# A third Strassen level in five more pairs of steps

## The chip, the cores and the metric

The kernel runs on one core of a Trainium2 chip. The metric is the device time in microseconds of one execution. TensorE (PE in the profile) does the matmuls, VectorE (DVE) and ScalarE (ACT) work on its results in PSUM, GpSimd (POOL) adds and subtracts tiles in SBUF and issues some DMAs, and SyncE (SP) issues most of the DMAs.

## The reference

All data are float32. `x` is 32 samples x 128 channels x 2048 positions. Two blocks follow each other, each added to its input:

```python
# block 0: per-sample channel mix, then a wide linear layer
h    = gelu(gelu(cond @ W0 + b0) @ W1 + b1)
att  = softmax(h @ W2 + b2)                        # 8 expert kernels
mix  = einsum('bk,koi->boi', att, weight)          # 128 x 128 for each sample
y    = einsum('boi,bih->boh', mix, x) + att @ bias_k
W'   = W + sum_e coeffs_e * scales_e * Bf_e @ A_e  # 2048 x 2048, 16 updates of rank 16
x    = x + y @ W'.T + bias                         # the reference adds the updates apart
# block 1: grouped convolution, then 16 small FFNs over permuted positions
z    = conv1d(x, 4 groups, 9 taps) + ctx + fside
t    = z[:, :, perm] in 16 heads of 128
x    = x + unpermute(gelu(t @ up) @ down)          # 128 -> 512 -> 128
```

The channel mix and the linear layer commute, so the kernel multiplies `x` by `W'` first (2048 x 2048 with 4096 rows) and mixes the channels of the product afterwards.

## The kernel before

The product with `W'` is the largest part: it fills the first half of the time. The rows of `x` (4096 = 32 samples of 128) are cut into 8 groups g = 0 to 7 of 4 samples, 512 rows each. The product is computed in Strassen's (Winograd's) form at two or three levels:

- **Rounds.** At the outer level the 2048 x 2048 product is 7 products of half size, the rounds `ROUNDS = P1, P2, P6, P7, P5, P3, P4`. Each round goes over the 8 groups: 56 *steps* i = (round r, group g).
- **Second level.** Within a step, `multiply` computes seven products named P1 to P7 again. Each is 4 matmuls of 128x128 weights against 512 columns that add up in one PSUM bank (L346). Products share banks: P1, P6, P7 and P4 add up in `px`, P5 and P3 in `py`, P2 has `pz`; between two of them the bank is read out. Where a partial result of an earlier round was loaded, DVE adds each bank to it (L339); in round P1 there is none, and the first write of each quarter of the new tile `m_rg` is a copy by ACT (L341). At the end the tile is stored to DRAM (`part_store`, L274, issued on SP).
- **Third level.** For a *pair* of steps (g even, then g odd), `multiply_third` leaves the second level's products P2 and P4 out of both steps and computes them for both together by seven *quarter* products, each 4 matmuls of 256 columns (`quarter`, L449, its result added by DVE, L457), all in the odd step, scattered between the plain products (L438, L434). The even step's tile is held until the odd step has ended (`held`). The quarters need combined weights, made once in a round (`third_weights`: two tiles `r_q0`, `r_q1`; eight POOL operations of 128x256, L390 to L396, and four of DVE, L1109), and combined inputs, made once for each pair (`third_inputs`: one tile `sq_i`, four operations of 128x512, L416 to L419, on POOL, or on DVE for a round's first pair). Before the change 19 pairs have it: all four of P6, P7, P5 and P3 and three of P2 (`THIRD`, `SKIP`).

The first round does more than its products. `W'` is made in 16 blocks of 1 MB (`w_khohkc`): loaded by SP (`w_load`, L161, two blocks in each step for the next one), the rank-16 updates multiplied on TensorE and added by DVE (`w_make_two`, 14 matmuls of 512 columns for two blocks, L220 and L223, ahead of the products of steps 1 to 5), summed by rows on DVE (`row_sums`, L240), and stored for the later rounds by a DMA that POOL issues (`w_store`, L165, to `wb_d`). At the start POOL also makes P1's inner weights (`inner_weights`, L249 to L253). A *chain* of small steps for the second half (`small`) advances after each step: after step 6 DVE works out positions (L927 to L935) and transposes and reduces the weights' sums through a tile `wsq` (L945, L946).

The last round, P4, mixes the channels (ACT, POOL and DVE, L566 to L584) and runs the first parts of the convolution between its steps. The convolution (L673), and the 128 FFN heads (L817, L828) fill the second half.

What sets the order: the program is scheduled by hand. The order of the code is the order of instructions on each engine and each queue, and an engine never passes a waiting instruction. In each step's code, first the next step's x is loaded (`x_load`, L265, SP) and combined (`x_combine`, L308 to L311, POOL); then come the step's `W'` blocks and their stores; then its products, with `between(j)` called after the j-th for what is to lie among them; then the store of the result, and the chain.

Nearly all large tiles (x, `W'` blocks, combined weights and inputs, partial results, `wsq`, tables) share one pool of `SLOTS` = 25 buffers of 1 MB (128 partitions x 2048 floats):

```python
def slot(name, shape=(P, L)):
    return big.tile(list(shape), FP, name=name, tag="s")
```

A new tile gets the next buffer, and its first writer waits until all users of that buffer's former tile are done. PSUM has 8 banks, handed out in turn by `bank()` and given back by `done()`.

Of the kernel before, what the change touches and what calls it, by code (L numbers as in the profile page):

```python
# [11 lines left out]
ALU = mybir.AluOpType  # L12
# [4 lines left out]
P = 128  # L17
B = 32
L = 2048
QW = 512  # L20
# [7 lines left out]
NQ = QW // 2  # L28
# [19 lines left out]
ROUNDS = ("P1", "P2", "P6", "P7", "P5", "P3", "P4")  # L48


THIRD = ("P2", "P6", "P7", "P5", "P3")
SKIP = (("P2", 3),)


@with_exitstack
def adaln_ffn_kernel(
# [16 lines left out]
    nc = tc.nc  # L73
# [8 lines left out]
    def slot(name, shape=(P, L)):  # L82
        return big.tile(list(shape), FP, name=name, tag="s")


    def bank():
        return banks.pop(0)

    def done(*ps):
        banks.extend(ps)  # L90

    def halves(t):
        return [t[:, r * NQ : (r + 1) * NQ] for r in range(2)]
# [144 lines left out]
    def row_sums(oh, t):  # L238
        for ki in range(2):
            nc.vector.tensor_tensor(wsum[:, oh], wsum[:, oh], t[:, ki], ALU.add)  # L240
# [32 lines left out]
    def part_store(n, g, t, eng=nc.gpsimd):  # L273
        eng.dma_start(part_d[n, g], t.rearrange("p k s c -> p (k s c)"))  # L274
# [129 lines left out]
        return quarters, ops  # L404

    def in_pair(r, g):
        return r in THIRD and (r, g // 2) not in SKIP

    def third_inputs(i, eng):

        (x11, x12), (x21, x22) = (
            [xa[n][:, 1, :, h * NQ : (h + 1) * NQ] for h in range(2)] for n in (i, i + 1)
        )
        tt = eng.tensor_tensor
        t = slot(f"sq_{i}", (P, 4, 2, NQ))
        tt(t[:, 0], x21, x22, ALU.add)  # L416
        tt(t[:, 1], t[:, 0], x11, ALU.subtract)
        tt(t[:, 2], x11, x21, ALU.subtract)
        tt(t[:, 3], x12, t[:, 1], ALU.subtract)  # L419
        return {  # L420
            "P1": x11, "P2": x12, "P3": t[:, 3], "P4": x22,
            "P5": t[:, 0], "P6": t[:, 1], "P7": t[:, 2],
        }

    def multiply_third(r, g, lhs, rhs, olds, between, quarters, sq):

        px, py = bank(), bank()
        if sq:
            qx, qy, qz = bank(), bank(), bank()
            both = [held.pop(), olds]  # L430

        def add(si, oi, ps):
            for acc in olds:
                nc.vector.tensor_tensor(acc[:, si, oi], ps, acc[:, si, oi], ALU.add)  # L434

        def product(k, ps, first, last):
            for kc in range(4):
                nc.tensor.matmul(  # L438
                    ps, lhsT=lhs[k][:, bass.ts(kc, P)], rhs=rhs[k][kc],
                    start=first and kc == 0, stop=last and kc == 3, skip_group_check=True,  # L440
                )

        def quarter(k, ps, first, last, *to):

            if not sq:
                return
            for i, out in enumerate(halves(ps)):
                for kc in range(2):
                    nc.tensor.matmul(  # L449
                        out, lhsT=sq[k][:, i, bass.ts(kc, P)], rhs=quarters[i][k][kc],  # L450
                        start=first and i == 0 and kc == 0, stop=last and i == 1 and kc == 1,
                        skip_group_check=True,
                    )
            for b, h in to:
                for acc in both[b]:
                    part = acc[:, :, 0, h * NQ : (h + 1) * NQ]
                    nc.vector.tensor_tensor(  # L457
                        part, ps.rearrange("p (s n) -> p s n", s=2), part, ALU.add
                    )

        product("P1", px, True, False)
        add(0, 0, px)
        between(0)
        quarter("P1", qx if sq else None, True, False, (0, 0))
        quarter("P2", qz if sq else None, True, True, (0, 0))
        if sq:
            done(qz)
        product("P5", py, True, False)
        add(1, 1, py)
        between(1)  # L470
        quarter("P6", qx if sq else None, False, False, (0, 1))
        quarter("P5", qy if sq else None, True, False, (1, 1))
        product("P6", px, False, False)
        add(0, 1, px)
        between(2)
        quarter("P7", qx if sq else None, False, False, (1, 1))
        quarter("P3", qy if sq else None, False, True, (0, 1))
        if sq:
            done(qy)
        product("P3", py, False, True)  # L480
        add(0, 1, py)
        done(py)
        between(3)
        quarter("P4", qx if sq else None, False, True, (1, 0))
        if sq:
            done(qx)
        product("P7", px, False, True)
        add(1, 1, px)
        add(1, 0, px)
        done(px)  # L490
        between(4)
        between(5)
        if not sq:
            held.append(olds)
            return
        for b, accs in enumerate(both):
            for (_, new), acc in zip(ADDED[r], accs):
                part_store(new, g - 1 + b, acc, nc.sync)

    held = []  # L500
# [345 lines left out]
    def late_loads():  # L846
        late["tw"] = slot("tw_l", (P, 4, GR, P))
        nc.sync.dma_start(late["tw"].rearrange("p k r c -> p (k r c)"), tw_d)
        late["w1"] = slot("w1", (P, NPH, QW))
        nc.sync.dma_start(late["w1"].rearrange("p f n -> p (f n)"), w1_d.to_broadcast([P, L]))  # L850
        late["fb"] = slot("fb", (P, NPH, QW))
        nc.sync.dma_start(
            late["fb"].rearrange("p f n -> p (f n)"), fbias.to_broadcast([P, L])
        )
# [161 lines left out]
    first = [wt.pop(k) for k in blocks[0:4]]  # L1016
# [15 lines left out]
    rhs = inner_weights("P1", first, make_first)  # L1032
    a_load(1, 0, 4)
    unsummed, unsummed_first = [], list(first)
    olds = {}
    chain = small()
    nxt, waiting, ts = {}, {}, {}
    heads = [(g, h) for g in range(NG) for h in range(NH)]

    def olds_load(i):  # L1040
# [3 lines left out]
    for i, (r, g) in enumerate(steps):  # L1044
        ri = i // NG
        last_round = ri + 1 == len(ROUNDS)
        if i + 1 < len(steps):
            if i + 1 not in xs:
                xs[i + 1] = x_loads(*steps[i + 1])
            if not last_round:  # L1050
                lhs[i + 1] = x_combine(*steps[i + 1], xs.pop(i + 1))
                if r in THIRD and g == 0:
                    quarters, quarter_ops = third_weights(r, rhs)
                if in_pair(r, g) and g % 2 == 0 and g > 0 and r != "P6":
                    sq = third_inputs(i, nc.gpsimd)
# [7 lines left out]
        if g == NG - (1 if ri else 2) and ri < len(ROUNDS) - 1:  # L1063
            nxt = inner_weights(ROUNDS[ri + 1], [nxt[kc] for kc in range(4)])
# [18 lines left out]
        elif ri + 1 < len(ROUNDS):  # L1083
            for k, combine in waiting.items():
                nxt[k] = combine()
            waiting = {}
            if 2 <= g < 6:
                waiting[g - 2] = outer_weights(ROUNDS[ri + 1], g - 2)

        if last_round and g == 0:  # L1090
            late_loads()
        if last_round and g == 2:

# [6 lines left out]
        def between(j):  # L1100

            b = (ri - 1) * (NG - 2) + g + 1 if ri > 0 else g - (NG - 2)
            if (g in range(1, NG - 1) if ri > 0 else g >= NG - 2) and b < B and j < KEXP // 2:
                mixed_kernel(b, (2 * j, 2 * j + 1))
            if ri == 0 and j == 2:
                for k in blocks[6 + 2 * g : 8 + 2 * g]:
                    wt[k] = w_load(*k)
            if r in THIRD and j < 4 and quarter_ops:
                nc.vector.tensor_tensor(*quarter_ops.pop(0), ALU.subtract)  # L1109
            if j == 3 and ahead and steps[i + 2][0] == "P6":  # L1110
                xs[i + 2] = x_loads(*steps[i + 2])
            if ri == 0 and j in (1, 3) and unsummed:
                row_sums(*unsummed.pop())
            if ri == 0 and j == 5 and unsummed_first:
                t = unsummed_first.pop(0)
                tt = nc.vector.tensor_tensor
                tt(wsum[:, 0, 0], wsum[:, 0, 0], t[:, 0, 0], ALU.add)
                tt(wsum[:, 0], wsum[:, 0], t[:, 1], ALU.add)
            if last_round:
                if j == 3 and i + 1 < len(steps):  # L1120
                    lhs[i + 1] = x_combine(*steps[i + 1], xs.pop(i + 1))
                    olds_load(i + 1)
                if j == 4 and i + 2 < len(steps):
                    xs[i + 2] = x_loads(*steps[i + 2])
                if j in (2, 4):
                    stage(k0 + j // 2, stage_first)
                if j % 2:
                    stage_third(k0 + j // 2)
                else:
                    stage(k0 + j // 2, stage_second)  # L1130
# [5 lines left out]
        else:  # L1136
            multiply(r, g, lhs.pop(i), rhs, olds.pop(i), between)
        xa.pop(i - 1, None)
        if in_pair(r, g) and g % 2 == 0 and (g == 0 or r == "P6"):
            sq = third_inputs(i, nc.vector)  # L1140
        next(chain, None)
        if i > 5:
            next(chain, None)
# [5 lines left out]
        if g == NG - 1 and ri + 1 < len(ROUNDS):  # L1149
            rhs = nxt  # L1150
            nxt = {}
# [86 lines left out]
```

## Time and profile before

| | before |
|---|---|
| median of 3 runs | 2592.68 us (2592.53 to 2594.41) |
| profiled execution | 2592.81 us |
| its span in the trace | 2591.0 us (1.8 us lie around it) |
| mean granted TensorE clock | 0.999 |
| PE busy | 2579.3 us, 6926 matmul records |
| DVE busy | 1491.7 us |
| POOL busy | 1329.8 us |
| ACT busy | 532.8 us |

The groups of instructions that the change touches, with all their busy time (a matmul's record contains a modelled tail, so records overlap):

| group | records | mean |
|---|---|---|
| L438, plain products in steps of a pair, two of its groups | 608 and 512 | 592 ns |
| L346, plain products elsewhere, its largest group | 288 | 592 ns |
| L308, POOL, combining x, the first of its four operations | 56 | 1319 ns |
| L434, DVE, adding a bank to u | 192 | 686 ns |

A float32 matmul is two records. The time of an engine in the page is a mean over the span; the first round lies from 46 to 303 us, the rounds up to P4 from there to 1232.7 us.

### The profile page before, as it was taken

The numbers are of one execution on the slowest core, as the hardware profiler recorded it, in microseconds if no ns is written. First come the engines' busy times: TensorE is split into PE (matmuls) and PEld (weight loads), VectorE is DVE, ScalarE is ACT, GpSimd is POOL, SyncE is SP. The second block draws the span as 40 slices with busy tenths as digits, with TensorE's granted clock in tenths as the row PEclk, the third lists the DMA queues.
The fourth block names the chain that finished last, engine by engine and source line by source line (L and its number), as shares of the span: only waits on it lengthen the run. The fifth ranks groups of instructions, "written<-read, shape, count | busy, mean of one in ns | idle before, by whom it ended". The sixth has DMA issues, their size and how long they took to land. (4 is left out here: it accounts for less than half of the span.)

```text
span 2591.0 us, 21495 instructions
## 1 busy us (share of the span) xinstructions
PE 2579.3 (100%) x6926; PEld 1314.6 (51%) x6926; DVE 1491.7 (58%) x2345; ACT 532.8 (21%) x1099; POOL 1329.8 (51%) x1096
## 2 busy tenths in 40 slices
PE   9999999999999999999999999999999999999999
PEld 4444455455555555555454455555555555455543
DVE  5654655466554666654276666667666666666601
ACT  0000000000000000000011244444444444444432
POOL 7320657888977845977314234343344334434222
PEclk9999999999999999999999999999999999999999
DMA  7543458779467477573866897777777877787432
GB/s 324 210 171 115 156 230 319 305 295 353 169 253 288 195 319 288 208 318 146 279 203 228 246 304 260 244 247 226 220 234 239 254 237 221 222 257 231 163 128 89
DMA packets 186576, 608.28 MB, mean 235 GB/s; under 512 B 17632, under 2 KB 91872, under 8 KB 142304
## 3 DMA queue, kind: packets, MB, share of 16 engines
q1 hardware_dynamic: 147936, 473.48, 50.9%
q0 software_dynamic: 32704, 130.04, 14.8%
q10 hardware_dynamic: 5824, 3.40, 0.4%
q8 instruction: 55, 0.90, 0.1%
q14 instruction: 57, 0.47, 0.1%
HBM read 372.45 MB, written 200.84 MB: 221 GB/s over the span
## 5 line engine op out<-in xcount | busy, mean ns | idle before, releaser
L817 PE MATMUL bank<-t,ws 128*128 128x512 f32 x1024 | 460.6, 592 | 0.4 <-DMA ws<-in_ffw 0.4
L828 PE MATMUL bank<-gl,ws 128*128 128x512 f32 x1024 | 460.2, 592 | 0.0
L835 POOL DMA_INDIRECT out<-t,orow x128 | 150.3, 1174 | 552.9 <-DVE t L833 470.6
L820 ACT ACTIVATE gl<-bank 128x512 f32<-128x512 f32 x512 | 305.9, 598 | 418.7 <-PE bank L817 408.5
L828 PEld LDWEIGHTS bank<-gl,ws 128*128 128x128 f32 x1024 | 194.6, 190 | 233.0 <-issue 231.5
L817 PEld LDWEIGHTS bank<-t,ws 128*128 128x128 f32 x1024 | 194.4, 190 | 227.6 <-issue 224.2
L566 POOL TENSOR_TENSOR x<-x,fb 128x512 f32<-128x512 f32 x128 | 176.7, 1409 | 236.9 <-DMA x<-in_x 217.7
L833 DVE TENSOR_TENSOR t<-bank,t 128x512 f32<-128x512 f32 x128 | 88.4, 690 | 326.7 <-PE bank L828 320.6
L438 PE MATMUL bank<-P_t,s_P 128*128 128x512 f32 x608 | 270.2, 592 | 0.0
L572 ACT ACTIVATE bank<-w,aggb 128x512 f32<-128x512 f32 x128 | 80.9, 684 | 849.9 <-DMA w<-w_d 832.5
L434 DVE TENSOR_TENSOR u<-bank,u 128x512 f32<-128x512 f32 x192 | 125.9, 686 | 212.9 <-PE bank L438 197.6
L438 PE MATMUL bank<-wo_P,s_P 128*128 128x512 f32 x512 | 227.6, 592 | 0.0
L280 POOL TENSOR_TENSOR xt<-xt,xt 128x512 f32<-128x512 f32 x128 | 164.5, 1317 | 97.3 <-DMA xt<-in_xT 97.2
L308 POOL TENSOR_TENSOR s_P<-xt 128x512 f32<-128x512 f32 x56 | 73.8, 1319 | 234.7 <-DMA xt<-in_xT 231.7
L545 DVE SCALAR_TENSOR_TENSOR ags<-mix,att_bc,ags 128x128 f32<-128x128 f32 x224 | 179.5, 801 | 4.7
L438 PEld LDWEIGHTS bank<-P_t,s_P 128*128 128x128 f32 x608 | 115.5, 190 | 129.2 <-issue 125.3
L801 POOL DMA_INDIRECT t<-hx_d,row x128 | 131.0, 1023 | 55.2 <-issue 27.0
L438 PEld LDWEIGHTS bank<-wo_P,s_P 128*128 128x128 f32 x512 | 97.3, 190 | 108.8 <-issue 106.2
L346 PE MATMUL bank<-P_t,s_P 128*128 128x512 f32 x288 | 126.5, 592 | 0.0
L673 PE MATMUL bank<-va,tw_l 128*128 128x256 f32 x512 | 122.3, 380 | 2.7 <-DVE va L657 2.6
L434 DVE TENSOR_TENSOR p<-bank,p 128x512 f32<-128x512 f32 x84 | 56.6, 688 | 116.7 <-PE bank L438 112.2
L673 PEld LDWEIGHTS bank<-va,tw_l 128*128 128x128 f32 x512 | 96.7, 190 | 45.3 <-issue 33.3
(188 smaller groups left out, 3558.9 us busy)
## 6 DMA issues: line engine op xcount, KB each, us to landing
xt<-in_xT SPq DMA_DIRECT2D x88, 1024.0 KB
u<-u_d SPq DMA_DIRECT2D x40, 1024.0 KB
wo_P<-wb_d SPq DMA_DIRECT2D x36, 1024.0 KB
u<-c_d SPq DMA_DIRECT2D x64, 512.0 KB
x<-in_x SPq DMA_DIRECT2D x32, 1024.0 KB
xg<-x SPq DMA_DIRECT2D x256, 128.0 KB
hx_d<-x1t SPq DMA_DIRECT2D x32, 1024.0 KB
hx_d<-ht SPq DMA_DIRECT2D x32, 1024.0 KB
```

The source lines that it names most:

```text
L280: nc.gpsimd.tensor_tensor(out[:, i, j], a[:, i, j], b[:, i, j], op)
L346: nc.tensor.matmul(ps, lhsT=lhs[k][:, bass.ts(kc, P)], rhs=rhs[k][kc], start=first and kc == 0, stop=last and kc == 3, skip_group_check=True,)
L434: nc.vector.tensor_tensor(acc[:, si, oi], ps, acc[:, si, oi], ALU.add)
L438: nc.tensor.matmul(ps, lhsT=lhs[k][:, bass.ts(kc, P)], rhs=rhs[k][kc], start=first and kc == 0, stop=last and kc == 3, skip_group_check=True,)
L545: nc.vector.scalar_tensor_tensor(ag, mix[:, k], att, ag, ALU.mult, ALU.add)
L566: nc.gpsimd.tensor_tensor(xt[:, f], xt[:, f], late["fb"][:, f], ALU.add)
L673: nc.tensor.matmul(out, lhsT=w[:, 2 * i + r], rhs=rhs, start=first and r == 0, stop=last and r == 1, skip_group_check=True,)
L801: nc.gpsimd.indirect_dma_start(out=t.rearrange("p k t -> p (k t)"), out_offset=None, in_=hx_d[g].rearrange("l k t -> l (k t)"), in_offset= ...
L817: nc.tensor.matmul(pu, lhsT=w[:, m * P : (m + 1) * P], rhs=t[:, 0], start=True, stop=True)
L820: nc.scalar.activation(gl[m], pu, AF.Gelu)
L828: nc.tensor.matmul(pd, lhsT=w[:, (MC + m) * P : (MC + m + 1) * P], rhs=gl[m], start=(m == 0), stop=(m == MC - 1),)
L835: nc.gpsimd.indirect_dma_start(out=out, out_offset=bass.IndirectOffsetOnAxis(ap=orow[:, g, h : h + 1], axis=0), in_=t[:, 1], in_offset=None,)
```

## The change

`THIRD` and `SKIP` give way to a table `PAIRS` of the pairs that have the third level. New in it are all four pairs of round P1 and the first pair of P4: 24 pairs instead of 19. In P1 and P4 (`ENDS`) the seven quarter products of the odd step stand behind its plain products instead of between them, and the combined inputs are always made on GpSimd. Since P1 has no partial results to add to, `multiply_third` now also takes a new tile `m_rg` and has ACT copy first writes into it, as `multiply` did. PSUM banks for quarters are taken when the first quarter of a bank comes. In P4, `third_weights` is issued at the start of the round's first step, behind the x that was combined before. The code below leaves out the old calls of `quarter` and unchanged lines.

```diff
-THIRD = ("P2", "P6", "P7", "P5", "P3")
-SKIP = (("P2", 3),)
+PAIRS = {
+    "P1": (0, 1, 2, 3), "P2": (0, 1, 2), "P6": (0, 1, 2, 3), "P7": (0, 1, 2, 3),
+    "P5": (0, 1, 2, 3), "P3": (0, 1, 2, 3), "P4": (0,),
+}
+ENDS = ("P1", "P4")
...
     def in_pair(r, g):
-        return r in THIRD and (r, g // 2) not in SKIP
+        return g // 2 in PAIRS[r]
...
     def multiply_third(r, g, lhs, rhs, olds, between, quarters, sq):
         px, py = bank(), bank()
+        accs = olds if olds[0] is not None else [slot(f"m_{r}{g}", (P, 2, 2, QW))]
+        fresh = set()
         if sq:
-            qx, qy, qz = bank(), bank(), bank()
-            both = [held.pop(), olds]
+            both = [held.pop(), accs]
         def add(si, oi, ps):
-            for acc in olds:
-                nc.vector.tensor_tensor(acc[:, si, oi], ps, acc[:, si, oi], ALU.add)
+            for acc in accs:
+                to = acc[:, si, oi]
+                if olds[0] is not None or (si, oi) in fresh:
+                    nc.vector.tensor_tensor(to, ps, to, ALU.add)
+                else:
+                    nc.scalar.copy(to, ps)
+            fresh.add((si, oi))
...
+        turns = [
+            (("P1", (0, 0)), ("P2", (0, 0))), (("P6", (0, 1)), ("P5", (1, 1))),
+            (("P7", (1, 1)), ("P3", (0, 1))), (("P4", (1, 0)),),
+        ]
+        def turn(n, now):
+            if sq and now:
+                for k, to in turns[n]:
+                    quarter(k, to)
+        early = r not in ENDS
         product("P1", px, True, False)
         add(0, 0, px)
         between(0)
+        turn(0, early)
         product("P5", py, True, False)
         add(1, 1, py)
         between(1)
+        turn(1, early)
         product("P6", px, False, False)
         add(0, 1, px)
         between(2)
+        turn(2, early)
         product("P3", py, False, True)
         add(0, 1, py)
         done(py)
         between(3)
+        turn(3, early)
         product("P7", px, False, True)
         add(1, 1, px)
         add(1, 0, px)
         done(px)
+        turn(0, not early)
         between(4)
+        turn(1, not early)
+        turn(2, not early)
         between(5)
+        turn(3, not early)
...
-                if r in THIRD and g == 0:
+                if g == 2 * PAIRS[r][0]:
                     quarters, quarter_ops = third_weights(r, rhs)
...
         if last_round and g == 0:
+            quarters, quarter_ops = third_weights(r, rhs)
             late_loads()
...
-            if r in THIRD and j < 4 and quarter_ops:
+            if j < 4 and quarter_ops:
                 nc.vector.tensor_tensor(*quarter_ops.pop(0), ALU.subtract)
...
-        if in_pair(r, g) and g % 2 == 0 and (g == 0 or r == "P6"):
-            sq = third_inputs(i, nc.vector)
+        if in_pair(r, g) and g % 2 == 0 and (g == 0 or r == "P6" or last_round):
+            sq = third_inputs(i, nc.gpsimd if r in ENDS else nc.vector)
```

More of the change, by code (lines that the diff above doesn't have):

```diff
@@ L441, in product, with quarter @@
                 )
-        def quarter(k, ps, first, last, *to):
-            if not sq:
-                return
+        def quarter(k, to):
+            if k in ("P1", "P5", "P2"):
+                qs[k] = bank()
+            ps = qs[{"P6": "P1", "P7": "P1", "P4": "P1", "P3": "P5"}.get(k, k)]
+            first, last = k in ("P1", "P2", "P5"), k in ("P2", "P3", "P4")
             for i, out in enumerate(halves(ps)):
@@ L453, in quarter @@
                     )
[L454 to L459, printed above, removed]
+            b, h = to
+            for acc in both[b]:
+                part = acc[:, :, 0, h * NQ : (h + 1) * NQ]
+                nc.vector.tensor_tensor(
+                    part, ps.rearrange("p (s n) -> p s n", s=2), part, ALU.add
+                )
+            if last:
+                done(ps)
+        qs = {}
+        turns = [
[7 more added lines that the diff above has]
+        early = r not in ENDS
         product("P1", px, True, False)
@@ L463, in multiply_third @@
         between(0)
[L464 to L467, printed above, removed]
+        turn(0, early)
         product("P5", py, True, False)
@@ L470, in multiply_third @@
         between(1)
-        quarter("P6", qx if sq else None, False, False, (0, 1))
-        quarter("P5", qy if sq else None, True, False, (1, 1))
+        turn(1, early)
         product("P6", px, False, False)
@@ L475, in multiply_third @@
         between(2)
[L476 to L479, printed above, removed]
+        turn(2, early)
         product("P3", py, False, True)
@@ L483, in multiply_third @@
         between(3)
-        quarter("P4", qx if sq else None, False, True, (1, 0))
-        if sq:
-            done(qx)
+        turn(3, early)
         product("P7", px, False, True)
@@ L490, in multiply_third @@
         done(px)
+        turn(0, not early)
         between(4)
+        turn(1, not early)
+        turn(2, not early)
         between(5)
+        turn(3, not early)
         if not sq:
-            held.append(olds)
+            held.append(accs)
             return
@@ L1036, in adaln_ffn_kernel @@
     chain = small()
-    nxt, waiting, ts = {}, {}, {}
+    nxt, waiting, ts, quarter_ops = {}, {}, {}, []
     heads = [(g, h) for g in range(NG) for h in range(NH)]
```

## The prediction

> **What bounds the kernel now.** I read the busy shares first, then the waits of the engine that is always busy, then the timeline where the third level already runs, then the queues that hand out SBUF slots. The page:
>
> ```profile
> span 2591.0 us, 21495 instructions
> ...
> PE 2579.3 (100%) x6926; PEld 1314.6 (51%) x6926; DVE 1491.7 (58%) x2345; ACT 532.8 (21%) x1099; POOL 1329.8 (51%) x1096
> ...
> L438 PE MATMUL bank<-P_t,s_P 128*128 128x512 f32 x608 | 270.2, 592 | 0.0
> ```
>
> TensorE (PE) is busy for the whole span, and its matmuls show no idle time ahead of them. The waits of PE, in full, come to 5.4 us, none longer than 1.5:
>
> ```profile
> PE bank L673 <- DVE va L657: 2.6, 4, 0.7
> PE bank L154 <- DVE warm L151: 1.5, 1, 1.5
> PE bank L817 <- DMA ws<-in_ffw: 0.4, 1, 0.4
> PE bank L449 <- DVE u L457: 0.4, 1, 0.4
> ```
>
> So a matmul removed shortens the kernel by the time at which it is issued, and any new wait of PE lengthens it by its full length. Table of stretches, first round (46 to 303 us) and the end; columns are length, then busy time and count of PE, weight load, DVE, ACT, POOL, then the granted clock, DMA share, GB/s:
>
> ```profile
> 46.00:303.00 257.00, 256.83 (x609) 113.92 (x608) 138.00 (x188) 22.00 (x37) 86.82 (x74) 1.00 0.39 151
> 2584.80:2587.60 2.80, 0.00 (x0) 0.00 (x0) 0.69 (x1) 0.00 (x0) 0.97 (x1) 1.00 0.08 32
> 2587.60:2591.00 3.40, 0.00 (x0) 0.00 (x0) 0.00 (x0) 0.00 (x0) 0.00 (x0) 0.51 0.13 51
> ```
>
> The first round leaves DVE 119 and POOL 170 us idle; what it lacks is free slots, as will be seen. The other two rows serve the clock below.
>
> **Removed and added matmuls.** Each f32 matmul is two records. Their price is the distance of starts, not the mean of 592 ns, which holds a modelled pipeline tail. PE's timeline in P2's first pair:
>
> ```profile
> 332.99 3.60 PE L438 MATMUL bank<-P_t,s_P 128*128 128x512 f32 x8
> 336.42 1.89 PE L449 MATMUL bank<-P_q,sq 128*128 128x256 f32 x8
> 338.15 1.03 PE L449 MATMUL bank<-w,sq 128*128 128x256 f32 x4
> 339.01 1.03 PE L449 MATMUL bank<-P_t,sq 128*128 128x256 f32 x4
> ```
>
> Eight records of 512 columns take 336.42 - 332.99 = 3.43 us, 0.4288 each; sixteen of 256 take 339.87 - 336.42 = 3.45 (339.87 is the next start in that view), 0.2156 each. A pair loses 16 matmuls, 32 x 0.4288 = 13.72 us, and gains 28 of half width, 56 x 0.2156 = 12.07 us: 1.65 us less. Check by pairs that exist: stores of P2's pairs lie 387.21 - 340.79 = 46.42 us apart, and the plain steps of 253.31 to 301.46 take 48.15, 1.7 us less. Five new pairs: **-8.3 us** (8.25).
>
> Placement is free as such: seven quarters with nothing between them leave 1.72 us of matmuls between a bank's write and its next use, and the DVE add of 0.69 lies under it (without that cover 0.7 each).
>
> **New work beside PE.** P1 gets eight third-weight operations (6.9 us on POOL, 315.80 to 322.73 in P2), four of DVE, and four of inputs per pair on POOL (5.1 us, 1180.07 to 1185.2): 27 us against 170 us idle. As busy time it costs nothing; as order on POOL it costs much, because POOL also issues the stores of W' that free slots. All W' and x tiles share 25 slots of 1 MB; a new tile waits until its slot's last user is done. P1 now needs two weight tiles, an input tile and a second accumulator that it did not hold before. From the changed kernel's instruction order I read who waits for which slot; three places matter.
>
> *Step 1 (P1, group 1).* Its accumulator m_P11 takes the slot of weight block w_013. Its first write is ACT's copy of product P1, which waits until the store of w_013 has landed; and TensorE's third product, P6, goes into that same bank, so everything on PE stands behind it. The rows of before:
>
> ```profile
> 56.22 2.25 POOL L311 TENSOR_TENSOR s_P<-xt,s_P 128x512 f32<-128x512 f32 x1
> 58.41 1.10 POOL L165 DMA_DIRECT2D wb_d<-w  x2
> 59.50 0.23 POOL L874 MEMSET small<- 128x128 f32 x1
> 80.72 1.26 POOL L308 TENSOR_TENSOR s_P<-xt 128x512 f32<-128x512 f32 x1 [21.00 <-DMA xt<-in_xT]
> ```
>
> and for the store the landing row of tile wb_d:
>
> ```profile
> DMA to landing us min/median/max: 6.1/6.2/9.0
> ```
>
> Now third_weights stands between x1's combine and the first stores: 58.4 + 6.9 = 65.3; the second store is issued at 65.9 and lands at 72.1. The input quarters sq_0 take that slot: 72.1 + 5.6 = 77.7. Group 2's x takes the slot of the first store (landing 71.5) and needs 7.2 to 7.5 us (107.34 to 114.52, 302.77 to 310.32): 78.8. Its combine, 5.9 us (80.72 to 86.6), ends at 84.7; only then come the stores of w_012 and w_013, the second at 85.3, landing at 91.5; ACT's copy 0.6: 92.1. TensorE would want to start P6 at 46.0 (first multiply) + 20 x 0.8575 + 14 x 0.8575 (step 1's W' blocks) + 8 x 0.8575 = 82.0. **Stall 10.1 us**; with each leg at its short and long end 6.5 to 14.
>
> *Step 7 (P1, group 7).* m_P17 takes the slot of wsq, just freed. In before its slot had long been free. DVE:
>
> ```profile
> 274.20 0.69 DVE L339 TENSOR_TENSOR m_P<-bank,m_P 128x512 f32<-128x512 f32 x1 [2.67 <-PE bank L346]
> 274.81 0.41 DVE L927 TENSOR_SCALAR row<-pos 128x16 int32<-128x16 int32 x1
> ...
> 285.29 0.69 DVE L946 TENSOR_REDUCE small<-wsq 128x16 f32<-128x512 f32 x1
> ```
>
> The chain from 274.81 to 285.98, 11.2 us, follows step 6's last add, which ends about 0.85 us after TensorE has ended that step. So the copy of step 7's first product can run 12.0 us after that end and P6 0.6 later; TensorE wants it after 6.86. **Stall 5.8 us** (5 to 6.5: all its rows are of before).
>
> *Step 3.* The load of w_113 takes the slot of w_111, so it waits for that block's store, which POOL issues behind x3's combine and sq_2. From the start of step 2: x load issued at 2.3, 7.2 to 9.4 long (71.30 to 80.72 where two loads and a store share the queues); combine 5.1; sq 5.1 to 6; second store 0.6 and 6.2; load 6 to 7.3: 32.5 to 36.6, middle 34.6. Wanted at the sixth matmul of step 3's W' (12.0 + 17.15 + 4.3 = 33.5). **Stall 1.5 us**, 0 to 3.5.
>
> *P4's pair* adds weights on POOL (5.8 us, done about 1234.4) and inputs that are first used some 10 us after they are made; the step behind is 1.7 us earlier, while the mixing work before it is not. I take 0, up to 2. The other six waits that changed have margins from 0.5 us up (m_P16 for a store's landing is the nearest): 0.
>
> **Clock.** A stalled TensorE loses its clock: after the last matmul (2584.8) the granted clock is 1.00 for 2.8 us and then 0.51 (rows above). The price of coming back is seen at the start: 512-column records start 0.85 us apart (2.48, 3.33, 4.18) until 7.17, from 1.46; 5.7 us at half rate lose 2.85. Stalls 1 and 7 are longer than 2.8, so twice 2.85: **5.7 us**, bounds 0 (clock not dropped before work returns) and 5.7. Step 3's is too short.
>
> [...]
>
> **Sum.** 2592.8 (the profiled execution; span 2591.0 and 1.8 around it; the median 2592.7 differs by 0.1) - 8.3 + 10.1 + 5.8 + 1.5 + 5.7 = **2607.6 us**.
>
> **Rivals.**
> *Pure gain:* the slots come free in time, and only the matmuls count: 2592.8 - 8.3 = 2584.5, faster by 0.3%. For it: PE hides everything else here. It decides if w_013's store lands before 81.4 instead of 91.5 and wsq's reduces lie ahead of step 7; the legs of step 1 would have to be 10 us shorter out of 33, and their shortest rows give 3.6. Chance 0.05.
> *The stalls eat the gain:* shortest legs, no loss of clock: -8.3 + 6.5 + 5 = +3.2, 2596. Measurements of this kernel can tell about 0.2%, 5.2 us, from no change, so this is "same". For it: loads and stores meet emptier queues. Chance 0.09.
> *Long legs:* -8.3 + 14 + 6.5 + 3.5 + 5.7 + 2 (P4) = +23.4, 2616: POOL's operations run at 1.7 to 2.25 us beside DVE (56.22) instead of 1.27. Chance 0.2.
> *Quarters dearer than products:* by the mean records (592 and 379 ns) a pair would lose 56 x 0.379 - 32 x 0.592 = 2.3 us, five 11.4, and the whole be 2627. The starts in the timeline and P2's pairs speak against it: 0.02.
> The forecast itself has 0.64.
>
> **How the numbers follow.** Faster 0.05 (first rival); same 0.09 (second); slower 0.86 (the others). Below 2597 lie the first rival and part of the second (its middle is 2596, a little clock loss lifts it), some 0.1; above 2617 the fourth and the tail of the third, another 0.1.
>
> **What would show it.** In the changed profile: 160 fewer matmuls of 512 columns (320 records) and 280 more of 256; in PE's waits a bank released by ACT, near 10 us at about 82 us and near 6 us in step 7; in POOL's, waits for wb_d's landing ahead of sq_0; a granted clock of about 0.5 behind both. From P2's first step to P4 all stays as it was, shifted. The forecast is wrong if PE's waits in the first round stay below 5 us in sum, or if the rounds behind change length by over 2 us.

## The result, and the profile after

The changed kernel takes 2609.9 us (median of 6 runs, 2607.67 to 2611.48); the kernel before, in the same session, 2592.15. The ratio is 1.0069, 95% interval 1.0058 to 1.0080: slower by 0.7%. The forecast was 2607.6, within 2597 to 2617. The profiled execution took 2609.25 with a span of 2607.5, so 16.5 us more than the span before.

The page of the changed kernel:

```profile
span 2607.5 us, 21827 instructions
...
PE 2575.1 (99%) x7046; PEld 1338.0 (51%) x7046; DVE 1525.7 (59%) x2378; ACT 532.5 (20%) x1099; POOL 1377.1 (53%) x1132
...
L447 PE MATMUL bank<-P_t,s_P 128*128 128x512 f32 x768 | 344.9, 598 | 19.1 <-ACT m_P L442 19.1
```

TensorE has less to do (2575.1 us against 2579.3) and yet the span is longer: what was added is waiting. The mean of this group of the plain products' records has risen from 592 to 598 ns, a first sign of a slower clock. The waits of PE in the changed kernel (total, times, longest):

```profile
PE bank L447 <- ACT m_P L442: 19.1, 2, 13.0
PE bank L223 <- DVE w L226: 2.0, 2, 1.8
PE bank L693 <- DVE va L677: 2.0, 3, 0.7
```

The first row is most of the result: two waits of TensorE for a copy by ACT, 13.0 and 6.05 us. The second row holds a new wait of 1.8 us for DVE. PE's timeline at the three:

```profile
67.98 5.42 PE L223 MATMUL bank<-tb,sa 128*128 128x512 f32 x12 [1.80 <-DVE w L226]
...
96.72 5.91 PE L447 MATMUL bank<-P_t,s_P 128*128 128x512 f32 x8 [13.03 <-ACT m_P L442]
...
296.07 4.37 PE L447 MATMUL bank<-P_t,s_P 128*128 128x512 f32 x6 [6.05 <-ACT m_P L442]
```

The two long ones are P6 in steps 1 and 7, the product that shares its bank with P1. ACT shows what its copies wait for:

```profile
95.99 1.07 ACT L442 COPY m_P<-bank 128x512 f32<-128x512 f32 x2 [30.31 <-DMA wb_d<-w]
...
295.34 1.07 ACT L442 COPY m_P<-bank 128x512 f32<-128x512 f32 x2 [10.84 <-DVE small L966]
```

The copy in step 1 waits for the store of a W' block to land, the one in step 7 for the last reduce through wsq. POOL shows why that store was late; the rows are the last of third_weights, the first stores, the first operations of sq_0 and of x2's combine, and the store that ACT waits for (the second of its row):

```profile
67.87 0.72 POOL L399 TENSOR_TENSOR P_q<-w,P_q 128x256 f32<-128x256 f32 x1
68.54 1.10 POOL L168 DMA_DIRECT2D wb_d<-w  x2
76.32 1.26 POOL L419 TENSOR_TENSOR sq<-xt 128x512 f32<-128x512 f32 x1 [6.68 <-DVE w L226]
...
83.33 2.10 POOL L311 TENSOR_TENSOR s_P<-xt 128x512 f32<-128x512 f32 x1
...
89.14 1.10 POOL L168 DMA_DIRECT2D wb_d<-w  x2
```

The store is issued at 89.71 and lands at 95.84, and the copy starts at 95.99. The clock, in the table of stretches (the column behind the five engines is the granted clock):

```profile
83.50:87.00 3.50, 0.20 (x1) 0.00 (x0) 0.80 (x1) 0.00 (x0) 3.42 (x3) 1.00 0.00 0
88.00:96.00 8.00, 0.00 (x0) 0.00 (x0) 0.00 (x0) 0.01 (x1) 7.22 (x7) 0.50 0.64 262
96.00:101.00 5.00, 4.28 (x5) 1.85 (x6) 0.00 (x0) 1.07 (x2) 0.00 (x0) 0.50 0.00 0
```

It halves about 4 us into the wait of step 1 and stays at 0.50 for the first matmuls behind it.

### The profile page after: what moved, and what is told of

It is laid out like the page before. It is cut to its first block, busy times and chain, and to the rows that moved or that the text cites. A ratio compares the mean times of both kernels' runs of the same rounds, so it can differ in the third digit from the quotient of the medians.

```text
span 2607.5 us, 21827 instructions
## 1 busy us (share of the span) xinstructions
PE 2575.1 (99%) x7046; PEld 1338.0 (51%) x7046; DVE 1525.7 (59%) x2378; ACT 532.5 (20%) x1099; POOL 1377.1 (53%) x1132
## 5 line engine op out<-in xcount | busy, mean ns | idle before, releaser
L447 PE MATMUL bank<-P_t,s_P 128*128 128x512 f32 x768 | 344.9, 598 | 19.1 <-ACT m_P L442 19.1
L440 DVE TENSOR_TENSOR u<-bank,u 128x512 f32<-128x512 f32 x204 | 134.0, 687 | 230.8 <-PE bank L447 212.0
L447 PEld LDWEIGHTS bank<-P_t,s_P 128*128 128x128 f32 x768 | 147.3, 192 | 189.5 <-issue 185.6
L447 PE MATMUL bank<-wo_P,s_P 128*128 128x512 f32 x544 | 241.6, 592 | 0.0
L447 PEld LDWEIGHTS bank<-wo_P,s_P 128*128 128x128 f32 x544 | 103.4, 190 | 116.5 <-issue 113.8
L460 PE MATMUL bank<-P_q,sq 128*128 128x256 f32 x576 | 131.4, 379 | 0.4 <-DVE u L468 0.4
L460 PEld LDWEIGHTS bank<-P_q,sq 128*128 128x128 f32 x576 | 109.3, 190 | 31.9 <-issue 17.5
L693 PE MATMUL bank<-va,tw_l 128*128 128x256 f32 x512 | 122.1, 380 | 2.1 <-DVE va L677 2.0
L447 PE MATMUL bank<-wo_P,xt 128*128 128x512 f32 x272 | 122.3, 592 | 0.0
```

The costliest lines, as they stand in the source:

```text
L440: nc.vector.tensor_tensor(to, ps, to, ALU.add)
L447: nc.tensor.matmul(ps, lhsT=lhs[k][:, bass.ts(kc, P)], rhs=rhs[k][kc], start=first and kc == 0, stop=last and kc == 3, skip_group_check=True,)
L460: nc.tensor.matmul(out, lhsT=sq[k][:, i, bass.ts(kc, P)], rhs=quarters[i][k][kc], start=first and i == 0 and kc == 0, stop=last and i == 1 ...
L693: nc.tensor.matmul(out, lhsT=w[:, 2 * i + r], rhs=rhs, start=first and r == 0, stop=last and r == 1, skip_group_check=True,)
```

## The experiments

**e1: the stores of W' on another queue.** It tells whether POOL's order is what delays step 1.

```diff
-            w_store(k, t)
+            w_store(k, t, nc.scalar)   # in w_make_two; w_store takes the queue
```

> The stores of the W' blocks made in steps 0 to 5 are issued on ACT's queue instead of POOL's; all else is as in the changed kernel. Theory (the store of w_013 is late because POOL issues it behind third_weights, sq_0 and the combine of x2): ACT can issue it right after DVE's last add to the block, at about 77.6 us of the changed trace instead of 89.7, so with the 6.1 us of that row it lands at about 83.8; TensorE wants its bank at 83.5, so the wait of 13.0 us falls below 2 and the loss of clock behind it (2.3 us) goes with it: span 2592 to 2594 against 2607.5. The wait in step 7 (6.05 us, for wsq) stays. Rival (the slot is not the cause, TensorE is held up by POOL and DVE having more to do in P1): the wait stays above 8 us and the span above 2603.

2594.31 us, ratio 1.0010 (1.0001 to 1.0020), span 2592.2. PE's waits, and ACT in step 1:

```profile
PE bank L447 <- ACT m_P L442: 7.6, 2, 6.0
```

```profile
76.56 1.19 ACTq L168 DMA_DIRECT2D wb_d<-w  x2
84.35 1.07 ACT L442 COPY m_P<-bank 128x512 f32<-128x512 f32 x2 [18.84 <-DVE wsum L243]
```

The 13.0 us are 1.6 now, and the 6.0 of step 7 are unchanged. So the late store was the cause, and POOL's order made it late. A quicker queue is not what helped: in e9, the run with this edit whose landings can be read, the stores on ACT's queue land 3.9 to 7.2 us after their issue in steps 1 to 5, those on POOL's in the changed kernel 4.2 to 6.8. What is next late in that slot shows too: the copy now waits for DVE's row_sums, the last reader of the same block. The rival, a wait above 8 us, is out.

**e2: wsq's stage ahead of the positions.**

```diff
 after step 6:
-   row, orow (L947 to L955)
    wsq: 4 transposes, 4 reduces (L965, L966)
+   row, orow
```

> Two stages of the chain behind step 6 change places on DVE: the transposes and reduces through wsq come first, the positions (row, orow) second; all else is as in the changed kernel. Theory (ACT's copy in step 7 waits for wsq's last reduce): that reduce ends 5.9 us earlier, the copy runs about when TensorE wants the bank, so the wait of 6.05 us falls to 0 to 0.6, the clock is not lost there (1.6 us), and the span is 7 to 7.8 us shorter: 2599.7 to 2600.5. The wait in step 1 stays 13. Rival (the copy waits for DVE's whole queue, or for the store of an earlier tile): the wait stays within 1 us of 6.

2602.13 us, ratio 1.0043 (1.0027 to 1.0058), span 2600.5.

```profile
PE bank L447 <- ACT m_P L442: 13.8, 2, 13.0
...
PE bank L460 <- DVE m_P L468: 0.8, 1, 0.8
```

Step 7's wait fell from 6.05 to 0.8, a little above the 0 to 0.6 of the theory, and the span is at the upper end of what it gave; a small new one of 0.8 stands before a quarter, whose bank DVE reads late.

**e3: both.** The diff is e1's and e2's.

> Both edits together: W' stores of steps 0 to 5 on ACT's queue, wsq's stage ahead of the positions. Theory: both waits go, what remains is five pairs at 1.65 us less each, the 1.8 us that TensorE now waits for DVE ahead of step 1's W' blocks, and at most 1 us in step 1: 2591.0 - 8.25 + 1.8 + (0 to 1) = 2584.6 to 2585.6 us span, about 0.2% faster than the kernel before. Rival (the quarters behind the plain products cost time of their own, not only waits for slots): the span stays at or above 2591.

2589.05 us, ratio 0.9990 (0.9981 to 0.9999), span 2589.8: just faster than the kernel before, but 4.2 us short of the expectation. Part of that is the execution that was profiled: it is the slowest of eleven (2591.56), and the median one has a span of 2587.3, 1.7 us short. The profiled one's waits:

```profile
PE bank L693 <- DVE va L677: 3.7, 5, 0.8
PE bank L447 <- ACT m_P L442: 2.3, 2, 1.6
PE bank L223 <- DVE w L226: 2.0, 2, 1.8
...
PE bank L460 <- DVE m_P L468: 0.8, 1, 0.8
```

I had summed 1.8 and "at most 1"; there are 2.0, 2.3 and 0.8 in the first round, and the convolution (L693) waits 1.1 us longer for DVE than before. Counted over all matmuls as the distance of starts less 0.429 us (512 columns) or 0.2156 (256), TensorE loses 19.4 us here and 11.9 in the trace of before: 7.5 more, against 8.25 less to do, and its last matmul starts 0.75 us earlier (2583.45 against 2584.20). Such a count closes by its making; what it tells is where the loss lies. The 224 quarter records of P1 lose 1.2 us in all, of which 0.96 is the one wait for DVE; in the changed kernel they lose 0.14. So the quarters behind the plain products cost next to nothing of their own, and the rival is out.

**e4: third_weights behind the first stores.** A test of the chain's length instead of its existence.

```diff
-                if g == 2 * PAIRS[r][0]:        # ahead of the step's W' blocks
+                if ri > 0 and g == 2 * PAIRS[r][0]:
 ...
                 made.extend(ks)
+                if g == 0:
+                    quarters, quarter_ops = third_weights(r, rhs)
```

> In P1 the eight POOL operations of third_weights are issued behind the stores of w_010 and w_011 instead of ahead of them. Theory (chain of step 1: third_weights, store, landing, sq_0, x2's combine, store, landing): the first stores go out at about 59 us instead of 68.5 and land at about 66 while POOL does third_weights (60 to 69.7); then sq_0 (6.9) and the combine of x2 (5.8) end at 82.4, the second store lands at 89.1 instead of 95.8: the wait in step 1 falls from 13.0 to 6.4 us (5.5 to 7.5). Rival (the second pair of stores is late for another reason, such as the load of x2 or the queues): the wait stays above 10 us.

2602.42 us (one run), span 2600.6; PE waits for ACT 10.9 us in two, of which 5.9 in step 7, so 5.0 in step 1, where 6.4 was expected and 5.5 to 7.5 allowed. POOL:

```profile
59.71 1.10 POOL L168 DMA_DIRECT2D wb_d<-w  x2
...
73.99 1.27 POOL L422 TENSOR_TENSOR sq<-xt,sq 128x512 f32<-128x512 f32 x1
...
81.36 1.10 POOL L168 DMA_DIRECT2D wb_d<-w  x2
```

The second pair of stores goes out at 81.4 instead of 89.1 (the expectation had 82.4), because sq_0 ran at 1.27 us per operation here (5.1 in all) and not in 6.9. The chain holds; its lengths vary with how fast POOL's operations run. A wait of 1.9 us that the changed kernel has at 0.2 stands ahead of step 3's blocks here.

**e5: P4's pair alone.** `"P1": ()` in PAIRS.

> Of the five new pairs only P4's first is left; P1 has none. Theory (a pair that meets no wait for a slot gains what its matmuls cost less, 1.65 us): span 2591.0 - 1.65 + (0 to 0.9, a wait of TensorE for DVE in step 53 or so that the changed kernel's trace shows as 0.6 and e3_both as 0.7) = 2589.3 to 2590.3, no wait of TensorE for ACT in the first round. Rival (quarters behind the plain products cost time of their own): span above 2591.

2587.35 us, ratio 0.9987 (0.9978 to 0.9996), span 2585.3: faster by 1.0 to 5.7 us, where 1.65 was expected, which the interval holds. The profiled span is 5.7 us below that of before and below the 2589.3 to 2590.3 expected, more than the pair can give. The rest is not in P4's stage: counted as in e3, TensorE loses 2.2 us from the first matmul of the convolution on, and 5.7 in the trace of before. The same count is 2.1, 2.8, 5.7 and 7.5 in e9, e10, the changed kernel and e3, which all have this pair, so that part isn't the pair's. What moves it was not settled; a trace is one execution, and those of one kernel differ by as much (before, beside e5: 2588.75 to 2592.34).

**e6: P1 without pair 0.** `"P1": (1, 2, 3)`.

> P1 has its pairs 1, 2 and 3 but not pair 0, so third_weights moves to step 2; P4's pair stays. Theory: step 1 then holds no second accumulator and no input quarters, and its wait is gone with the clock lost behind it; m_P17 still waits for wsq's last reduce in step 7: about 6 us and 1.6 of clock. Span 2591.0 - 4 x 1.65 + 7.8 = 2592.2, 2591.5 to 2594. Rival (the wait in the first steps belongs to third_weights wherever it stands): a wait of 5 us or more moves to step 2 or 3, span above 2597.

2599.72 us (one run), span 2597.9. Here the rival's number was right:

```profile
PE bank L447 <- ACT m_P L442: 6.0, 1, 6.0
PE bank L223 <- DVE w L226: 5.4, 2, 5.2
```

Step 1's wait is gone, but one of 5.2 us stands in step 3, where TensorE waits for DVE and DVE for a load. SP and POOL in step 2:

```profile
111.34 28.53 SPq L164 DMA_DIRECT2D w<-in_WT  x2
```

```profile
118.99 1.18 POOL L393 TENSOR_TENSOR P_q<-w 128x256 f32<-128x256 f32 x1
...
132.78 1.10 POOL L168 DMA_DIRECT2D wb_d<-w  x2
```

third_weights and sq_2 (119.0 to 132.8) stand ahead of the stores of w_110 and w_111, the second of which frees the slot of w_113; that block's load goes out only at 139.6. It is the chain that the prediction priced at 1.5 us for step 3, with third_weights added to it.

**e7: matmuls that fill the wait.**

```diff
+        if (r, g) == ("P1", 1):
+            pd = bank()
+            for n in range(15):
+                nc.tensor.matmul(pd, lhsT=lhs["P1"][...], rhs=rhs["P1"][n % 4], start=True, stop=True)
+            done(pd)
         product("P6", px, False, False)
```

> The changed kernel with fifteen extra matmuls (12.9 us) into a free PSUM bank in step 1, right ahead of product P6, where TensorE waits 13.0 us; their result is not used. They lie inside the wait and cost nothing themselves. Theory (the wait halves the clock and the matmuls behind it pay 2.3 us): the granted clock stays at 1.00 there, the matmuls behind start every 0.43 us, the remaining wait is below 1 us, and the span is 2607.5 - 2.3 = 2605.2 (2604.7 to 2605.7). Rival (the slow matmuls behind the wait have another cause, such as the work that piled up): they are slow here too and the span stays at 2607.5.

2606.32 us (one run), span 2603.6. PE's timeline and the stretch behind the wait:

```profile
83.34 13.04 PE L497 MATMUL bank<-w,xt 128*128 128x512 f32 x30
96.56 3.67 PE L447 MATMUL bank<-P_t,s_P 128*128 128x512 f32 x8 [0.19 <-ACT m_P L442]
```

```profile
96.00:100.00 4.00, 3.81 (x9) 1.63 (x9) 0.00 (x0) 0.91 (x2) 0.00 (x0) 1.00 0.00 0
```

With 12.9 us of extra work the kernel is not longer (one run). The eight records behind last 3.67 us instead of 5.91 and the granted clock is 1.00: 2.2 us, near the 2.3 expected, are the price of the lost clock at that wait. The span fell by 1.7 us more than that, below the range; by the same count TensorE loses 2.1 us less in the convolution and the FFN, which is of the kind seen in e5, and 1.0 more to the clock behind step 7's wait.

**e8: the last waits of e3.** e3's edits, with wsq's stage moved to step 5, and

```diff
-            if j < 4 and quarter_ops:
+            if j < 4 and quarter_ops and i > 0:
```

> The edits of e3_both, with two more: wsq's stage of the chain stands behind step 5 instead of step 6 (ahead of the context's and the positions' stages), and P1's four DVE operations for the quarter weights are done in step 1 instead of step 0. Theory: the waits that e3_both still has in the first round (1.8 us for DVE ahead of step 1's W' blocks, 1.6 in step 1 for a slot that DVE's row_sums hold, 0.7 and 0.8 in step 7) shrink to 0 to 1.5 in all, so that the four pairs of P1 give back their 6.6 us: span 2591.0 - 8.25 + (0.5 to 2.5) = 2583.3 to 2585.3, 0.2 to 0.3% faster than before. Rival (DVE is simply too full in P1 for the pairs' adds): these waits come back at other places, span 2588 or more.

2591.67 us, ratio 1.0004 (0.9995 to 1.0014), span 2589.2. A miss: the waits came back elsewhere and the span is above 2588, as the rival had it.

```profile
PE bank L460 <- DVE m_P L468: 6.0, 1, 6.0
```

```profile
92.83 0.69 DVE L1128 TENSOR_TENSOR P_q<-P_t 128x512 f32<-128x512 f32 x1 [14.21 <-PE bank L447]
```

The waits ahead of step 1's blocks are nearly gone (0.5 in two), but in step 1 the moved operations themselves waited for TensorE until 92.8, just after its first quarter began at 92.56, and with them DVE's row_sums and adds behind them, up to the adds of the first quarters; the next quarter, which uses their bank, then waited 6.0 us. The rival's reason, a full DVE, is not what the row shows. DVE was held: it stood idle for 14 us and then had everything at once. Why these operations waited so long was not traced further.

**e9 and e10: three pairs of P1, with the queues in order.** `"P1": (1, 2, 3)`, e1's stores, and wsq's stage behind step 5 (e9) or as in e2 (e10).

> P1 has its pairs 1, 2 and 3 (not 0), P4 its first; the W' stores of steps 0 to 5 are issued on ACT's queue; wsq's stage of the chain stands behind step 5. Theory (three pairs of P1 gain their 1.65 us each once no wait for a slot is left: e6's wait of 5.2 us in step 3 is for the load of w_113, whose slot is freed by a store that POOL issues behind third_weights and sq_2, and ACT issues it some 20 us earlier): against e5_p4_only (span 2585.3) 3 x 1.65 less and 0 to 2 of small waits more: 2580.3 to 2582.3. Rival (the load of w_113 is late for itself, or DVE is too full): a wait of over 3 us stays in steps 2 to 4, span 2585 or more.

> As e9_three_pairs, but wsq's stage stands behind step 6, ahead of the positions, as in e2 and e3. Theory: e2 and e3 show 0.7 and 0.8 us of waits in step 7 with it, which e8 does not have in that step; so 0 to 1.5 us longer than e9. Rival (which place wsq has does not matter once its reduce comes first): within 0.3 us of e9 in the waits of step 7.

e9: 2583.27 us, ratio 0.9969 (0.9957 to 0.9981), span 2581.5, inside the range expected; e10: 2584.82, ratio 0.9974 (0.9964 to 0.9984), span 2583.2. PE's longest waits in e9, and SP in step 2:

```profile
PE bank L447 <- ACT m_P L442: 0.8, 1, 0.8
PE bank L223 <- DVE w L226: 0.7, 2, 0.5
```

```profile
111.59 13.56 SPq L164 DMA_DIRECT2D w<-in_WT  x2
```

The load of w_113 goes out at 124.8 instead of 139.6, and the wait in step 3 is 0.5 at most: e6's reading holds. e10 keeps 1.0 us before a quarter in step 7 that e9 does not have, as its theory said, but the two intervals overlap. e9 is faster than the kernel before by 0.3% and than the changed kernel by 1%: the change was worth making in four of its five pairs, once the stores of W' no longer stood behind the work that it brought and wsq's reduces came earlier. The two edits of order were not run without the new pairs. They can have given little there: in the trace of before TensorE has 0.2 us of waits in the whole first round.

## Why the prediction was right

The mechanism held, and the two places that make up most of the sum; one place was left out, one came to almost nothing, and the sizes differ. Measured from start to start in the changed kernel's trace:

| step of the sum | forecast | measured | from |
|---|---|---|---|
| matmuls | -8.3 | -8.25 by count; P4's part 83.20 to 81.56 | start of the convolution less the first store of P3's last pair |
| step 1 | 10.1 | 13.2 | first matmul behind the wait, less 0.43 |
| step 7 | 5.8 | 6.2 | the same |
| step 3 | 1.5 | 0.2 | the same |
| clock | 5.7 | 3.9 (2.31 and 1.63) | late starts behind both waits |
| DVE ahead of step 1's blocks | 0 | 2.0 | first matmul behind the wait, less 0.43 |

The sum is 17.2 against 14.8; other waits came out 0.7 us shorter than in the trace of before, which gives the 16.5 of the spans. That the forecast came within 2.3 us of the result is partly luck: terms that were 5.5 us too small in all (step 1, step 7, DVE) stand against terms 3.1 too large (step 3, clock).

- **The price of a pair** held, and so did taking starts and not means: by the means a pair would have lost 2.3 us, and five of them 11.4. One sentence of the prediction was wrong beside a right sum: five pairs are 80 matmuls of 512 columns less and 140 of 256 more, that is 160 and 280 records; it called these numbers matmuls.
- **Step 1** was right in its chain but for one link, and 3 us short in length. The link is x2's load: it landed at 80.9, before sq_0 had ended at 83.2, so POOL did not wait for it. The view puts POOL's wait ahead of sq_0 down to an add by DVE, where the prediction looked for a store's landing; that store landed at 75.80, half a microsecond before sq_0 began, and in e4 sq_0 began at 70.2 while the same adds ran on to 77.8, so it does not wait for them. POOL's operations were taken mostly from rows where they ran undisturbed: third_weights took 9.5 us (59.0 to 68.5) for 6.9, sq_0 6.9 for 5.6, the x combine before them ended 0.6 later. Beside DVE's operations in SBUF the 128x256 ones ran at 1.2 to 1.7 us instead of 0.72:

```profile
65.01 1.24 POOL L399 TENSOR_TENSOR P_q<-w,P_q 128x256 f32<-128x256 f32 x1
66.21 1.70 POOL L399 TENSOR_TENSOR P_q<-w,w 128x256 f32<-128x256 f32 x1
67.87 0.72 POOL L399 TENSOR_TENSOR P_q<-w,P_q 128x256 f32<-128x256 f32 x1
```

 The slow rows (1.17 to 1.71 us, five in a row from 60.54 on) stand beside DVE's last quarter operation (60.03 to 61.13), its row_sums (61.05 to 64.46) and wsum adds (64.98 to 67.3), the fast one at 67.87 beside DVE's adds from a bank (67.25 on). Why they were slower was not shown.
- **Step 7** was read from rows of before alone, and came within 0.4 us.
- **Step 3** waited 0.2 us, at the short end of its 0 to 3.5. The chain is there in the changed kernel's trace: step 2 starts at 121.56, the stores go out at 142.5 and 143.0, the second lands at 149.81, the load of w_113 is issued at 149.87 and lands at 154.71, 33.15 us after the step's start. The forecast had 34.6: x3's load and that of w_113 (4.84 for 6 to 7.3) were shorter, sq_2 (6.9 for 5.1 to 6) longer. Its sum also held two slips: 34.6 less the 33.5 at which TensorE wants the block is 1.1, not 1.5, and the long legs add to 36.9, not 36.6. In e6 third_weights stands in this chain as well, and the wait is 5.2.
- **The wait for DVE** ahead of step 1's W' blocks is the term that the prediction left out. DVE's rows:

```profile
60.03 1.10 DVE L1130 TENSOR_TENSOR P_q<-P_t,P_q 128x512 f32<-128x512 f32 x1
61.05 3.41 DVE L243 TENSOR_TENSOR wsum<-wsum,w 128x1024 f32<-128x1024 f32 x2
...
67.25 4.30 DVE L226 TENSOR_TENSOR w<-bank,w 128x512 f32<-128x512 f32 x7
```

 The prediction counted DVE's four new operations in step 0 as free, by the busy share of the whole round; but step 0 is 6.9 us shorter on TensorE without its P2 and P4, and DVE's row_sums and adds there were pushed behind the next blocks' first banks. The four took 1.1 to 1.75 us each there, beside POOL's operations, and 0.7 in e8; an add of the same size in the changed kernel, at 151.64, where POOL was idle, took 0.68. e8, which takes the four out of step 0, has 0.4 of the 2.0 left.
- **The clock** was lost at both waits, as foreseen, but the way back cost 2.31 and 1.63 us, not 2.85. In e4, e6 and e7, waits of 5 to 6 us cost 1.6 to 2.6; the row of the start lies outside that.

## What to carry to other kernels

Where tiles share a rotating pool and the code's order is the queue's order, price a new tile by the tile whose slot it takes: follow that slot back to the last user, and that user back along its queue. Work that "lies beside" a full engine is only free if nothing that the full engine waits for stands behind it on the same queue; moving a store to an idle queue can be worth more than the arithmetic saved (e1: 15.3 us of span against 8.25). And a stage's slack must be read in its own step: a round in which DVE is half idle had a step in which it was late.

## What the hardware showed that was not expected

A wait of 13 us cost 15.5, because the granted clock fell to 0.50 after about 4 us and the records behind the wait started 0.85 to 0.99 us apart for 4.4 us; behind the wait of 6 us they did so for about 3 us. In the ten waits of 5 to 13 us of these runs the granted clock fell 2.5 to 5.4 us after the start of the wait (in e4 just after the next matmul had begun); waits of up to 2.1 us did not lower it (at the 2.0 of the changed kernel ahead of 67.98 it stays at 1.00). Filling the wait of 13 us with unused matmuls took back 2.2 us of the lost clock (e7). Two stores of 1 MB issued together by POOL landed 4.2 us (the first) and 6.1 us (the second) after their issues in the changed kernel (89.14 to 93.35, 89.71 to 95.84).
